# A four-block gated transformer kernel: the cell's sums closed in two planned pieces, queries spread ahead of keys, the first values stored by GpSimd, constants issued behind the gates

## The chip, the cores and the metric

The kernel runs on one core of one Trainium2 chip, in one launch. The metric is the time of an execution on the device in microseconds (us); lower is better.

The names used below: TensorE (PE) multiplies matrices, with its weight loads shown as PEld; VectorE is DVE, ScalarE is ACT, GpSimd is POOL, and SyncE is SP, which here only issues DMAs. SBUF is the on-chip memory, PSUM the accumulator memory that TensorE writes.

## The reference, cut to what matters

Eight sequences of 512 tokens with 256 features pass through four residual blocks, all in float32:

```
x += tanh(g0) * mlstm(layernorm(x), ctx, ctx)          # "cell": 8 heads of 32
x += tanh(f0) * moe_block(layernorm(x))                # self-attention, 32 heads of 8, then 8 experts
x += tanh(g1) * cross_attention(ctx, ctx, layernorm(x))# 16 heads of 16
x += tanh(f1) * product_key_ffn(layernorm(x))          # 4096 experts, top 8 of 64 x 64 per head
```

The cell, for one sequence and head, is

```
ig, fg = gates of [q, k, v];  cs = cumsum(log_sigmoid(fg))
log_D  = cs[s] - cs[t] + ig[t]  for t <= s, else -inf
m      = max_t log_D
C      = (q @ k.T / sqrt(32)) * exp(log_D - m)
h      = (C / (max(|sum_t C|, exp(-m)) + 1e-6)) @ v
out    = layernorm(h over 256 features) * ln_scale
```

The batch norm inside the product-key block takes its mean and variance over all tokens of all sequences, so that block can only start once all eight sequences have left the third one.

## The kernel before, in words

There are two stages. The attention stage (`attention_phase`) does the first three blocks for all sequences, and some matrix products of the fourth ahead. The second stage does the rest of the fourth block.

The attention stage has one backbone: 24 attention jobs of 16 steps. A job ("A", m, f) is one half of the self-attention of the m-th sequence, a job ("C", m, 0) is a cross-attention. Each job is worked through twice: first the maxima (products `sc<-ka,qa`, then a reduction `nm` on VectorE at line 440), then the exponentials (products `sc<-qa,ka`, then `pr` on ScalarE at line 469, then the products `av` at line 485). Normally the maxima of one job and the exponentials of the job before it run in the same step, and each step has two halves. The products of a half have two PSUM buffers (`ps_sc`), so the next half's products must wait until the reduction and the exponential of this half have read theirs. The operands of a job lie in one of three sets (`sets`, tiles `qa` and `ka`), whose rows are filled by `spread` (line 387) with DMAs from a DRAM copy of the projections (`qk_d`). `blank` (line 396) zeroes a row of the queries.

All other work of the attention stage is written as generators, called lanes. A lane yields a cost in planner's microseconds ("this much TensorE work was just issued"), `("wait", t)` ("do not call me for t planner's microseconds"), `("rest", name)` ("not before this name is in the set `rested`") or `("take", True/False)`, which holds or frees the one PSUM bank shared by cell and experts (`ps_ac`, tag "ac"). Behind each half, `beside` (line 1342) calls the first lane that can run until a credit of one or two planner's microseconds is used up. TensorE's instructions stand in exactly the order in which this program issues them (`manual_schedule` with ORDERED). The order on the other engines, SP's DMA queue included, is set by a scheduler, which `tc.issue_after` can hold back.

The lanes that matter here:

- `before` (line 1247) does cell and queries of a sequence. One lane does sequences 0, 2, 3, ... 7 with the tiles of `Tiles`; a second does sequence 1 with the borrowed tiles of `Lent`. Sequence 2 rests on ("cell", 1), which is set when the whole cell of sequence 1 is through.
- `between` (line 1263) calls `begin` (line 957) for each sequence: it rests on ("qk", m), then spreads queries and keys into the set, blanks, and later loads the values `v0` from `vds`.
- `behind` does experts and cross-attention operands, `contexts` keys and values of the cross-attention, `after` what follows it, and `fill` the early products of the fourth block.

`cell` (line 713) works, for sequences 1 to 7, on four pairs of heads one after the other. For each pair it makes the decays (GpSimd line 823, ScalarE line 831), the scores `csc` (line 853), their product with the decays (VectorE line 858) and the sums `cav` (line 838). Then `close` (line 774) copies the sums from PSUM to the SBUF tile `avs` (tag "pk", two buffers, shared with the tiles that carry projections out), transposes `avs` in four pieces into `ht` (line 780), and normalizes on VectorE (lines 785 to 792). For sequence 0, with nothing else to run, `all_pairs` (line 629) does the same in a tighter form and calls the same `close`.

`queries` (line 895) normalizes, projects queries and keys and stores them to `qk_d` through SP (line 927), then projects values and stores them to `v_d` through SP (line 943).

At the start, `lns` (line 281), the scale of the cell's normalization times tanh(g0), is made right after its load, and `constants` (line 324, called at line 739) prepares value tiles, bias and mask.

Of the kernel before, what the change touches and what calls it, by code (L numbers as in the profile page):

```python
# [16 lines left out]
ALU = mybir.AluOpType  # L17
# [19 lines left out]
def kernel(  # L37
# [27 lines left out]
    nc = tc.nc  # L65
# [13 lines left out]
    tg = const.tile([P, 4], F32, name="tg")  # L79
# [100 lines left out]
    def attention_phase(ctx: ExitStack):  # L180
# [97 lines left out]
        lns = cst.tile([P, D], F32, name="lns")  # L278
        nc.scalar.dma_start(lns, ln_scale.partition_broadcast(P))

        nc.vector.tensor_scalar(lns, lns, tg[:, 0:1], None, ALU.mult)


        tbo = cst.tile([P, D], F32, name="tbo")
# [38 lines left out]

        def constants():

            for f in range(2):
                nc.gpsimd.memset(v0[f], 1.0)
            nc.gpsimd.memset(v1, 0.0)
            bo_ps = ps_m.tile([P, S], F32, name="bo_ps", tag="m")
            for k in range(NK):  # L330
                nc.tensor.matmul(
                    bo_ps[:, :D], bqkv_sb[:, 4 + k : 5 + k].to_broadcast([P, P]), wo[:, k, :],
                    start=(k == 0), stop=(k == NK - 1),
                )
            nc.vector.tensor_tensor(tbo, bo_ps[:, :D], tbo, ALU.add)
            nc.vector.tensor_scalar(tbo, tbo, tg[:, 2:3], None, ALU.mult)
            m_f = trp.tile([B * NC, P], F32, name="m_f", tag="pk", bufs=2)
            nc.vector.tensor_copy(m_f, m_u8)
            mp = ps_m.tile([P, S], F32, name="mp", tag="m")
            nc.tensor.transpose(mp[:, : B * NC], m_f, ident[: B * NC, : B * NC])  # L340
            nc.vector.tensor_copy(m_key, mp[:, : B * NC])
            nc.vector.tensor_scalar(m_f, m_f, 1.0, -NEG, ALU.subtract, ALU.mult)
            nc.sync.dma_start(m_dram, m_f)
# [369 lines left out]
        def cell(m, own, loaded):  # L713
# [18 lines left out]
            z, a = rows[:, 1], rows[:, 0]  # L732
            for i, g in ((1, z), (0, a)):
                part = slice(32 * i, 32 * i + 8)
                nc.vector.tensor_scalar(g, gp[part], gb_sb[part], None, ALU.add)
            yield ("take", False)
            yield 0.9
            if m == 0:
                constants()

            nc.scalar.activation(e, z, AF.Abs)
            nc.scalar.activation(e, e, AF.Exp, scale=-1.0)
# [28 lines left out]

            hk = own.tokens("hk")

            def close(pair, av):

                avs = trp.tile([P, S], F32, name="avs", tag="pk", bufs=2)
                nc.any.tensor_copy(avs, av)
                ht = ps_m.tile([P, NC, 2, 2, 32], F32, name="ht", tag="m")
                for c in range(NC):
                    nc.tensor.transpose(  # L780
                        ht[:, c].rearrange("p i w r -> p (i w r)"), avs[:, c * P : (c + 1) * P],
                        ident,
                    )
                dn = small.tile([P, NC, 2], F32, name="dn")
                nc.vector.scalar_tensor_tensor(
                    dn, ht[:, :, :, 1, 0], -1.0, em[:, :, 2 * pair : 2 * pair + 2],
                    ALU.mult, ALU.max,
                )
                nc.vector.tensor_tensor(dn, dn, ht[:, :, :, 1, 0], ALU.max)
                nc.vector.tensor_scalar(dn, dn, EPS_CELL, None, ALU.add)  # L790
                nc.vector.reciprocal(dn, dn)
                nc.vector.tensor_tensor(
                    hk[:, :, 64 * pair : 64 * pair + 64].rearrange("p c (i r) -> p c i r", i=2),
                    ht[:, :, :, 0, :],
                    dn.unsqueeze(3).to_broadcast([P, NC, 2, 32]),
                    ALU.mult,
                )

            if m == 0:
                all_pairs(qT, cT, ce, nM_d, aT, close)  # L800
            mbs = {}

            def fetch_maximum(pair):
# [5 lines left out]
            for pair in range(4) if m else ():  # L809

                if pair not in mbs:
                    fetch_maximum(pair)
                    yield ("wait", 2.5)
                mb = mbs[pair]
                if own.ahead and pair < 3:
                    fetch_maximum(pair + 1)
                g = pair // 2
                pds = {}

                def decay(c):  # L820
                    s0 = c * P

                    nc.gpsimd.affine_select(  # L823
                        out=mb[:, :, s0 : s0 + P], in_=mb[:, :, s0 : s0 + P],
                        pattern=[[0, 2], [1, P]], compare_op=ALU.is_ge,
                        fill=NEG, base=0, channel_multiplier=-1,
                    )
                    pds[c] = own.pair()
                    for i in range(2):
                        h = 2 * pair + i  # L830
                        nc.scalar.activation(  # L831
                            pds[c][:, i, s0:], mb[:, i, s0:], AF.Exp, bias=aT[:, c, h : h + 1]
                        )

                def sums(c):
                    for i in range(2):
                        h = 2 * pair + i
                        nc.tensor.matmul(  # L838
                            av[64 * i : 64 * i + 64, c * P :],
                            ce[:, c, 33 * h : 33 * h + 64],  # L840
                            pds[c][:, i, c * P :], start=(c == 0), stop=(c == NC - 1),
                        )

                decay(0)
                yield ("wait", 1.5)
                yield ("take", True)
                av = own.bank("cav")
                for c in range(NC):
                    s0 = c * P
                    sc = [ps_m.tile([P, S], F32, name="csc", tag="m") for _ in range(2)]  # L850
                    for i in range(2):
                        r = 32 * (2 * (pair % 2) + i)
                        nc.tensor.matmul(
                            sc[i][:, s0:], cT[r : r + 32, g, s0 : s0 + P], qT[r : r + 32, g, s0:],
                            start=True, stop=True,
                        )
                    for i in range(2):
                        nc.vector.scalar_tensor_tensor(  # L858
                            pds[c][:, i, s0:], sc[i][:, s0:], 1.0 / math.sqrt(32.0),
                            pds[c][:, i, s0:], ALU.mult, ALU.mult,  # L860
                        )
                    if c > 0:
                        sums(c - 1)
                    if c < NC - 1:
                        decay(c + 1)
                    yield 1.1 * (NC - c) / NC + (1.1 * (NC + 1 - c) / NC if c else 0)
                    yield ("wait", 1.5)
                sums(NC - 1)
                close(pair, av)
                yield ("take", False)  # L870
                yield 1.1
            Xa = own.stream()
            nc.gpsimd.dma_start(Xa, x[b].rearrange("(c p) d -> p c d", p=P))
            if m == 0:
# [20 lines left out]
        def queries(m, own, Xa):  # L895
# [21 lines left out]
            for i in range(2):  # L917
                w = weights1.get()
                for n in range(NK):
# [7 lines left out]
                        nc.sync.dma_start(pds[i][n * P : (n + 1) * P], pk)  # L927

                    yield from project_T(w, nT, n, store)
            rested.add(("qk", m))  # L930
            vds[m] = drm.tile([P, 2, NC, 16 * 9], F32, name="v_d", bufs=M)
            w = weights1.get()
            for c in range(NC):
                ps = project(w, nT, c)
                pk = trp.tile([P, S], F32, name="vk", tag="pk", bufs=2)[:, : 32 * 9]
                heads = pk.rearrange("p (h e) -> p h e", e=9)
                nc.gpsimd.memset(heads[:, :, 8], 1.0)
                for f in range(2):
                    nc.any.tensor_copy(
                        heads[:, 16 * f : 16 * f + 16, 0:8].rearrange("p (j g) e -> p j g e", g=4),  # L940
                        ps.rearrange("p (j f g e) -> p j f g e", f=2, g=4, e=8)[:, :, f],
                    )
                nc.sync.dma_start(
                    vds[m][:, :, c], pk.rearrange("p (f n) -> p f n", f=2)
                )
                yield 1.0
# [10 lines left out]
        def begin(m):  # L957
            for f in range(2):
                i, last = block2_set(m, f)
                yield ("rest", ("qk", m))  # L960
                if last is None and i:
                    prepare(i)
                if last:
                    yield ("rest", last)
                for half, src in zip(sets[i], qks[m]):
                    spread(half, src, 32 * f, 8)
                blank(sets[i][0])
                yield ("wait", LANDING)
                ready.add(("A", m, f))
                yield ("rest", ("v_d", m))  # L970
# [276 lines left out]
        def before(sequences, tiles):  # L1247
            own, loaded = tiles(), None
            if tiles is Lent:
                loaded = own.begin(sequences[0])  # L1250
                yield ("rest", ("qk", 0))
            for m in sequences:
                if m == 2:
                    yield ("rest", ("cell", 1))
                Xa = yield from cell(m, own, loaded)
                rested.add(("cell", m))
                yield from queries(m, own, Xa)
            if tiles is Lent:
                rested.add(("lent", 0))
# [558 lines left out]
    for g, (p, u) in enumerate(steps):  # L1818
        n, step = g // 8, g % 8
        q = p + 2  # L1820
# [101 lines left out]
```

## Time and profile before

| | |
|---|---|
| times of three runs | 3832.28, 3841.15 and 3819.53 us, median 3832.28 |
| the profiled execution | 3834.04 us, of which the span in the trace is 3832.3 us |
| mean granted TensorE clock | 0.969 of full speed |
| first attention product starts at | 103.81 us |
| closings of the cell, transposes `ht` of cells 1 to 7 | 112 in 28 groups of four, 306 ns each on average |
| copies `avs` | 23 on VectorE (0.68 us typically), 9 on ScalarE (0.56 to 0.59 us) |

How to read it: times in the trace count from the start of the span. Each line of an order of time gives start and duration in us, the engine, the source line, the operation, and what it writes and reads; in square brackets stands how long the engine had been idle before it, and what ended that idle time. A line of a table of waits names the waiting engine and line, what it waited for, then the total in us, the number of times and the longest. A line of windows gives the stretch and its length, then busy us and the number of instructions of PE, PEld, DVE, ACT and POOL, then granted clock, DMA share and GB/s.

### The profile page before, as it was taken

To read this page: it belongs to the slowest core of one execution; us is meant where nothing else is said; L and a number is where in the kernel's file an instruction comes from. 1 tells how busy PE (TensorE), PEld (TensorE's weight loads), DVE (VectorE), ACT (ScalarE), POOL (GpSimd) and SP (SyncE) were. 2 spreads that over 40 slices of the span, in tenths; PEclk is the share of its full clock that TensorE was granted. 3 is DMA by queue.
4 is the path that set the end of the run, shared out by engine and by line. 5 is a ranking of instruction groups with operands and counts; after the bars stand their busy time and mean duration, and the time that the engine had idled before them with its cause. 6 is when DMAs were issued, how large, how long until landed. Compare 5 with 4: busy or idle time off the path is not lost. (4 is left out here: it accounts for less than half of the span.)

```text
span 3832.3 us, 76234 instructions
## 1 busy us (share of the span) xinstructions
PE 3520.6 (92%) x31049; PEld 1837.9 (48%) x31049; DVE 2241.0 (58%) x5490; ACT 1758.3 (46%) x2301; POOL 598.4 (16%) x642
## 2 busy tenths in 40 slices
PE   4788888998999999899999999999899999999998
PEld 2332333443343344334433444434345777777776
DVE  4665555565555555555555543545422689999993
ACT  2125453444445444445445444444443455555551
POOL 3130102121100101101100110100000133333331
PEclk8889999999999999999999999999999999999999
DMA  4331222233322323321332243330434433333331
GB/s 140 104 105 51 63 55 65 59 96 77 97 87 64 87 68 101 87 87 56 104 92 64 71 105 98 92 100 24 136 114 146 124 112 107 107 107 107 107 105 37
DMA packets 226092, 345.35 MB, mean 90 GB/s; under 512 B 25983, under 2 KB 174495, under 8 KB 217439
## 3 DMA queue, kind: packets, MB, share of 16 engines
q1 hardware_dynamic: 207884, 278.02, 24.5%
q0 software_dynamic: 16672, 61.87, 5.4%
q8 instruction: 244, 4.00, 0.4%
q14 instruction: 108, 0.88, 0.1%
q10 hardware_dynamic: 1184, 0.58, 0.1%
HBM read 238.50 MB, written 101.09 MB: 89 GB/s over the span
## 5 line engine op out<-in xcount | busy, mean ns | idle before, releaser
L440 DVE TENSOR_REDUCE nm<-sc 128x2 f32<-128x1024 f32 x768 | 938.7, 1225 | 968.2 <-PE sc L422 967.5
L469 ACT ACTIVATE pr<-sc 128x1024 f32<-128x1024 f32 x768 | 782.8, 1023 | 952.8 <-PE sc L422 952.4
L422 PE MATMUL sc<-ka,qa 32*128 32x512 f32 x3072 | 918.0, 662 | 109.0 <-DVE nm L440 102.9
L422 PE MATMUL sc<-qa,ka 32*128 32x512 f32 x3072 | 866.5, 652 | 17.4 <-ACT pr L469 15.5
L422 PEld LDWEIGHTS sc<-ka,qa 32*128 32x128 f32 x3072 | 250.6, 188 | 458.3 <-DVE nm L440 266.6
L1764 PE MATMUL acc<-up_sb,gs 64*128 64x256 f32 x4096 | 467.9, 381 | 1.3 <-DVE gs L1753 1.3
L131 PE MATMUL ps_hd<-xT,dw 128*64 128x256 f32 x3584 | 435.3, 388 | 14.5 <-DVE pd L858 4.5
L485 PE MATMUL av<-pr,v 128*32 128x512 f32 x3072 | 422.3, 622 | 2.4 <-DMA v<-v_d 2.3
L1764 PEld LDWEIGHTS acc<-up_sb,gs 64*128 64x128 f32 x4096 | 389.8, 187 | 52.2 <-issue 4.9
L131 PEld LDWEIGHTS ps_hd<-xT,dw 128*64 128x64 f32 x3584 | 246.9, 138 | 237.1 <-issue 100.7
L1734 POOL TENSOR_TENSOR m<-o,cwT 128x1024 f32<-128x1024 bf16 x128 | 243.6, 1903 | 581.4 <-DVE o L1732 260.9
L1210 ACT COPY hb<-ps_hd 128x512 f32<-128x512 f32 x224 | 130.9, 585 | 321.2 <-PE ps_hd L131 294.6
L422 PEld LDWEIGHTS sc<-qa,ka 32*128 32x128 f32 x3072 | 234.0, 185 | 53.3 <-ACT pr L469 40.7
L485 PEld LDWEIGHTS av<-pr,v 128*32 128x32 f32 x3072 | 61.3, 109 | 300.5 <-issue 297.1
L831 ACT ACTIVATE pd<-mb,aT 128x512 f32<-128x512 f32 (+1 forms) x224 | 113.5, 554 | 145.7 <-PE cav L838 86.9
L1753 DVE TENSOR_TENSOR gs<-cf,gs 128x1024 f32<-128x1024 f32 x128 | 155.6, 1217 | 41.9 <-PE cf L1744 27.2
L823 POOL TENSOR_SCALAR_AFFINE_SELECT mb<-mb 128x256 f32<-128x256 f32 x112 | 45.3, 406 | 724.9 <-ACT pd L831 407.6
L1744 PE MATMUL cf<-m,m 64*64 64x64 f32 x8192 | 153.1, 222 | 2.7 <-issue 2.0
L1744 PEld LDWEIGHTS cf<-m,m 64*64 64x64 f32 x8192 | 135.3, 135 | 40.8 <-issue 40.4
L1730 ACT CAST m<-o 128x1024 f32<-128x1024 bf16 x128 | 133.7, 1044 | 39.0 <-DVE o L1728 35.2
L1008 PE MATMUL ps_h<-fT,w1e 128*128 128x256 f32 x512 | 135.5, 397 | 8.5 <-DVE o L513 8.0
L1027 PE MATMUL ps_y<-w2e,heT 128*128 128x256 f32 x512 | 131.9, 397 | 0.0
(262 smaller groups left out, 4025.0 us busy)
## 6 DMA issues: line engine op xcount, KB each, us to landing
h_d<-hb SPq DMA_DIRECT2D x224, 256.0 KB
gs<-h_d SPq DMA_DIRECT2D x56, 1024.0 KB
dw<-in_down SPq DMA_DIRECT2D x112, 256.0 KB
w1e<-in_w POOLq DMA_DIRECT2D x16, 1024.0 KB, 5.5
w2e<-in_w POOLq DMA_DIRECT2D x16, 1024.0 KB, 6.5
mb<-nM_d SPq DMA_DIRECT2D x28, 512.0 KB
cT<-in_cxT POOLq DMA_DIRECT2D x22, 512.0 KB, 4.7
qk_d<-pk SPq DMA_DIRECT2D x32, 256.0 KB
```

The lines of the kernel that those rows point to most:

```text
L131: nc.tensor.matmul(ps[64 * q : 64 * q + 64, :], dw[:, k, :], runs[:, :, q, :], start=(k == 0), stop=(k == NK - 1),)
L422: nc.tensor.matmul(sc[:, i, :], lhs[r : r + 32, g, c * P : (c + 1) * P], rhs[r : r + 32, g, :], start=True, stop=True,)
L440: newest = nc.vector.tensor_reduce(self.nm[:, c, 2 * half : 2 * half + 2, g], sc, AX.X, ALU.max, negate=True)
L469: nc.scalar.activation(mine[jj], sc, AF.Exp)
L485: nc.tensor.matmul(self.av[32 * j : 32 * j + 32, :], self.va[:, c, h * (self.hd + 1) : h * (self.hd + 1) + 32], pr[j // 2][:, j % 2, :], s ...
L1008: nc.tensor.matmul(ps[:, :D], w1e[:, k, f * P : (f + 1) * P], fT[:, k, i * D : (i + 1) * D], start=(k == 0), stop=(k == NK - 1),)
L1027: nc.tensor.matmul(py[:, c, :], hT[:, f, c * P : (c + 1) * P], w2e[:, f, :], start=(f == 0), stop=(f == NF - 1),)
L1730: nc.scalar.copy(m1, o1)
L1734: nc.gpsimd.tensor_tensor(m2, o2, tokens(cw), ALU.mult)
L1744: nc.tensor.matmul(cf[64 * q : 64 * q + 64, h, s, :], m2[rows, 4 * q + s // 2, :, s % 2], m1[rows, 4 * q + s // 2, :, s % 2], start=True, ...
L1753: nc.vector.tensor_tensor(gv, cf.rearrange("p h s i -> p i h s"), gv, ALU.mult)
L1764: nc.tensor.matmul(accs[n][q], gs[n % 2][rows, i, :], up_sb[rows, i, :], start=(i == 0), stop=(i == 63),)
```

## The change: what it does

Five edits:

1. `close` is cut in two. `store_sums` copies the sums to `avs`; `close` does transposes and normalizer. For sequences 1 to 7 the lane yields between the two (cost 0.4, then a wait of 1.0), and the shared bank is freed behind the copy as before. Sequence 0 calls both in a row.
2. ("cell", m) is set behind the third pair of the cell (pair 2) instead of behind the whole cell, so the lane of sequence 2 may begin earlier.
3. The projections of queries and keys set ("q", m) and ("k", m) one after the other instead of ("qk", m) behind both. `begin` spreads and blanks the queries behind the first, and spreads the keys behind the second.
4. The values of sequence 0 are stored by a DMA from GpSimd instead of SP.
5. The multiplication of `lns` moves into `constants`, and `constants` is issued behind the second gate's addition (`gated`).

```diff
-        nc.vector.tensor_scalar(lns, lns, tg[:, 0:1], None, ALU.mult)
...
         def constants():
+            nc.vector.tensor_scalar(lns, lns, tg[:, 0:1], None, ALU.mult)
...
-                nc.vector.tensor_scalar(g, gp[part], gb_sb[part], None, ALU.add)
+                gated = nc.vector.tensor_scalar(g, gp[part], gb_sb[part], None, ALU.add)
...
             if m == 0:
-                constants()
+                with tc.issue_after(gated.ins):
+                    constants()
...
-            def close(pair, av):
-
+            def store_sums(av):
                 avs = trp.tile([P, S], F32, name="avs", tag="pk", bufs=2)
                 nc.any.tensor_copy(avs, av)
+                return avs
+
+            def close(pair, avs):
+
                 ht = ps_m.tile([P, NC, 2, 2, 32], F32, name="ht", tag="m")
...
             if m == 0:
-                all_pairs(qT, cT, ce, nM_d, aT, close)
+                all_pairs(qT, cT, ce, nM_d, aT, lambda pair, av: close(pair, store_sums(av)))
...
                 sums(NC - 1)
-                close(pair, av)
+                avs = store_sums(av)
                 yield ("take", False)
-                yield 1.1
+                yield 0.4
+                yield ("wait", 1.0)
+                close(pair, avs)
+                yield 0.7
+                if pair == 2:
+                    rested.add(("cell", m))
...
                     yield from project_T(w, nT, n, store)
-            rested.add(("qk", m))
+                rested.add(("qk"[i], m))
...
-                nc.sync.dma_start(
+                (nc.sync if m else nc.gpsimd).dma_start(
                     vds[m][:, :, c], pk.rearrange("p (f n) -> p f n", f=2)
                 )
...
-                yield ("rest", ("qk", m))
+                yield ("rest", ("q", m))
...
-                for half, src in zip(sets[i], qks[m]):
+                for half, src, name in zip(sets[i], qks[m], "qk"):
+                    yield ("rest", (name, m))
                     spread(half, src, 32 * f, 8)
-                blank(sets[i][0])
+                    if name == "q":
+                        blank(half)
...
-                yield ("rest", ("qk", 0))
+                yield ("rest", ("k", 0))
...
                 Xa = yield from cell(m, own, loaded)
-                rested.add(("cell", m))
                 yield from queries(m, own, Xa)
```

## The prediction

> **What bounds the kernel now.** I read the page first (busy shares, slices, chain), then windows of time, then what ends the idle time of TensorE, then the order of time at two places the change touches.
>
> ```profile
> span 3832.3 us, 76234 instructions
> PE 3520.6 (92%) x31049; PEld 1837.9 (48%) x31049; DVE 2241.0 (58%) x5490; ACT 1758.3 (46%) x2301; POOL 598.4 (16%) x642
> ...
> 0.00:104.00 104.00, 49.06 (x230) 25.66 (x231) 42.31 (x105) 27.30 (x54) 37.01 (x59) 0.81 0.46 136
> 104.00:150.00 46.00, 36.85 (x119) 17.18 (x120) 29.08 (x40) 8.22 (x13) 4.43 (x9) 0.69 0.41 106
> 150.00:250.00 100.00, 80.97 (x358) 38.11 (x357) 61.85 (x106) 20.43 (x37) 16.94 (x33) 0.83 0.28 85
> 250.00:500.00 250.00, 217.00 (x1340) 83.65 (x1336) 154.78 (x248) 116.78 (x151) 43.42 (x69) 0.97 0.23 69
> ```
>
> TensorE is the bound (92%). Its idle time is 312 us: 55 lie before 104 us, where the first attention product starts, and most of the rest in the attention stage up to 2680 us. There the waits of TensorE are:
>
> ```profile
> PE sc L422 <- DVE nm L440: 86.9, 158, 4.8
> PE ht L780 <- DVE avs L777: 26.5, 21, 1.9
> PE sc L422 <- ACT pr L469: 15.5, 15, 2.6
> PE ht L780 <- ACT avs L777: 7.6, 7, 1.7
> ```
>
> (us in total, times, longest, from 150 to 2680 us.) The second and fourth rows are one place in the code: the 28 closings of the cells 1 to 7, where the transposes `ht` stand directly behind the last sums, so that TensorE idles for the copy between them: 26.5 + 7.6 = 34.0 us (rounded rows), 1.21 us each. One of them in order of time:
>
> ```profile
> 341.57 1.23 DVE L440 TENSOR_REDUCE nm<-sc 128x2 f32<-128x1024 f32 x1 [1.12 <-PE sc L422]
> ...
> 342.03 0.44 PE L838 MATMUL cav<-pd,cte 128*64 128x128 f32 x4
> ...
> 342.87 0.63 DVE L777 COPY avs<-cav 128x512 f32<-128x512 f32 x1
> ...
> 343.56 0.66 PE L780 MATMUL ht<-ident,avs 128*128 128x128 f32 x4 [1.09 <-DVE avs L777]
> ...
> 344.14 0.69 PE L422 MATMUL sc<-ka,qa 32*128 32x512 f32 x1
> ```
>
> The start-up, by the two chains that the change meets:
>
> ```profile
> 13.10 0.35 DVE L281 TENSOR_SCALAR lns<-lns,tg 128x256 f32<-128x256 f32 x1 [5.26 <-DMA lns<-in_ln_scale]
> ...
> 14.27 1.14 ACT L228 COPY cte<-cx 128x512 f32<-128x512 f32 x2 [10.01 <-DMA cx<-in_cx]
> 15.43 1.31 ACT L360 COPY qT<-ps_t 128x512 f32<-128x512 f32 x2
> ...
> 92.09 0.32 SPq L927 DMA_DIRECT2D qk_d<-pk  x1
> 95.89 0.64 SPq L943 DMA_DIRECT2D v_d<-vk  x1
> 96.58 2.28 SPq L391 DMA_DIRECT2D qa<-qk_d  x3
> 98.91 1.79 SPq L391 DMA_DIRECT2D ka<-qk_d  x4
> ...
> 103.81 4.29 PE L422 MATMUL sc<-ka,qa 32*128 32x512 f32 x8 [5.28 <-DMA ka<-qk_d]
> ```
>
> **What the Trainium skill says.** Perfetto Trace Analysis, "Identifying the Most-Contended Engine", warns that matmul busy share does not show nearness to the roofline and asks for the share of weight loads too: here 92% beside 48%, so I count only gaps whose releaser is named. The same page, "Optimization Strategy", says a gap that repeats on the engine that should be saturated points at buffers or at what signals it; the 28 gaps of 1.21 us are such a series, and their releaser is a copy, not a missing buffer. DMA: Bandwidth & Descriptors, "Issuing engines are not separate DMA queues", says another issuing engine saves only issue time, since the transfers share the same DMA engines. The trace agrees on the size (0.64 us for the store) but shows more at stake: the store's place in SP's queue, behind a wait of 3.5 us. "Latency and other measured facts" of that page puts the fixed cost of a DMA near 2 us; here a `qk_d` store takes 4.6 us until its buffer is free (92.09 to the wait's end near 96.7), and 4.6 is used.
>
> **The change part by part.**
>
> 1. Constants behind the gates. The multiplication of `lns` stands ahead of the first normalization on VectorE and holds it to 13.37 us, though `rs` is ready at 9.69. Moving it frees 3.7 us there, but the next step, the copy of `qT`, follows on ScalarE's queue behind L228, which waits for `cx` and ends at 15.41. The copy starts at 15.43 either way: worth 0. Were `cx` early, up to 3.7. The constants' VectorE work then runs between 23.4 and 25.1 us, under the wait for the logarithm (25.90): 0.35 + 0.40 + 0.18 + 0.17 + 0.35 + 0.21 = 1.7 of 2.5 us. Cost 0.
>
> 2. Queries ahead of keys, values by GpSimd. In the new SP order the four query spreads stand in front of the second key store, the values are gone, then come the key spreads. The first two can go at 91.1; the other two need the second query store (87.70 + 4.6 = 92.3), so four at 0.39 end near 93.1. The second key store slips from 92.09 to 93.1, lands at 97.7, and only then go the last two key spreads: 97.7 and 98.1. Before, the last of four in 1.79 us went near 100.2. The first product moves up by about 2 us (103.8 to 101.8). Should spreads cost 0.76 each, as the three at 96.58 did, 0.5 us remains; with no contention 3. I take -2. The value stores on GpSimd have no row; nearest are its loads at 0.76 to 0.85 us issue and 5 us landing, so the fourth lands near 109, where the load of `v0` went before (109.27). SP waits there with the spreads of set 1 behind it, until about 113; set 1 is first read after the 16 steps of the first job, near 210 us, and `v0` by the first `av` at 244.6. Cost 0.
>
> 3. Copy and transposes in two pieces, 28 times. In the new TensorE order every `ht` of cells 1 to 7 has at least one group of attention products or four projections between it and the last sums, so the copy (0.63) is covered and the 34.0 us go. What is late next is the maxima (L440): the stall also gave VectorE time. In the example the reduction ends at 342.80 and the last sums at 342.47; without stall and `ht`, the next products start at 342.80: a wait of 0.33 replaces 1.09, so 0.76 of 1.09, 70%, is kept: 34.0 x 0.70 = 23.8 us. Bounds: none is kept if the maxima bind in each such half (0), or all of it plus `ht` itself filling gaps of about 0.42 us before products elsewhere (28 x 0.42 = 12): -46. I take -24.
>
> 4. Cell 2 may start after pair 2 of cell 1. Before the 64th group of four attention products 30 more other matmuls stand than before, where TensorE is only 80% busy; the total work is the same, and the last 82 groups of four products and all behind them stand in the same order. Attention steps that run with only one of the two kinds of product: 50 before, 48 after. The price for cell 1: counted in eights of attention products, its last key projection stands behind 18.5 of them instead of 17.5 (an eight takes some 6 us there), and job (A, 1, 0) needs it behind 22.5. Before, the spreads were issued by 295.1, landed by about 300, and the products began near 321: 20 us of room, so 14 remain. Cost 0, between -6 and +6 for the reshuffled order.
>
> Sum against the profiled span: 3832.3 - 2 - 24 = 3806. The run with the profile took 3834.0, the median of the three shown is 3832.3, so no correction is made.
>
> **Rivals.**
>
> A. The forecast: 3806, own range 3794 to 3818.
>
> B. The stall becomes a wait for the maxima. For it: L440 is already the largest releaser (86.9 us, 158 times), and a half-step with nothing beside it takes 2.47 us by that loop (346.70 to 349.17). Against: the new order puts other products into these halves. A quarter of the 34 kept and the 2 of the start: 3832 - 8.5 - 2 = 3822.
>
> C. The transposes fill gaps as well as lose theirs, and the early cell 2 fills the start: -46 at the extreme, about -38: 3794.
>
> D. Slower. The stall was the shadow in which VectorE did copy and normalizer; now the copy (0.63) and the chain of five small operations behind `ht` (344.25 to 345.51, 1.26) stand between two reductions. If every close falls into a half bound by the maxima it costs 28 x 1.89 = 53 us against 34 + 2 saved: +17, 3849, and more with a waiting `dn` ahead of a reduction. It outweighs the gain once more than 19 of 28 closes (36 / 1.89) lie in such halves. Only 158 of some 700 halves wait for the maxima today, and six of the copies move to ScalarE (23 to 17 on VectorE), so I hold it unlikely.
>
> That the change does not do what it says is excluded for the split (the order shows it) and is what I forecast for the constants.
>
> **How the numbers follow.** A 0.55, B 0.23, C 0.10, D 0.12. A change of 0.5% is 19 us, so faster means below 3813 and slower above 3851. A holds about 0.47 of faster, C 0.10, B 0.03 and measuring spread (the three runs lie within 22 us) leaves it there: 0.60 faster. Slower is the upper part of D, 0.09, where the spread of runs counts; the rest, 0.31, is within. The range takes A and C whole and B up to its upper end: 3790 to 3834.
>
> **What would show each step.** Right: TensorE's wait at `ht` for `avs` falls from 34 to under 4 us; the wait of L422 on L440 grows by about 10, not 30; the first product of `sc` at 101.8; `qT` copied at 15.4 still; no wait of products for `ka` of set 2. Wrong: L422 on L440 above 115 us (B, D); first products near 98 (constants mattered) or beyond 103; a gap on `ka<-qk_d` near 320. The forecast fails as a whole if TensorE's busy time itself moves, say by the granted clock.

## The result and the profile after

| | before | after |
|---|---|---|
| median, 16 runs each on the same chip | 3827.9 us | 3814.85 us |
| smallest to largest | 3818.01 to 3841.15 | 3803.85 to 3826.14 |
| span of the profiled run | 3832.3 us | 3820.4 us |
| TensorE idle in it (span less busy) | 311.7 us | 299.3 us |

The ratio is 0.9966, 95% interval 0.9953 to 0.9979: 13 us, about half of the gain that was forecast. It is a real gain (the interval excludes 1), and the median lies inside the forecast range of 3790 to 3834. But it is smaller than the 0.5% from which the prediction counts a kernel as faster, which it held more likely than not (0.60). The page of after:

```profile
span 3820.4 us, 76232 instructions
PE 3521.1 (92%) x31049; PEld 1833.6 (48%) x31049; DVE 2246.6 (59%) x5491; ACT 1756.5 (46%) x2300; POOL 600.5 (16%) x646
```

TensorE's busy time did not move (3520.6 before), so the 12 us between the two profiles are idle time of TensorE. The waits of TensorE in after from 150 to 2680 us (total, times, longest):

```profile
PE sc L422 <- DVE nm L440: 102.3, 169, 4.2
PE sc L422 <- ACT pr L469: 19.0, 16, 2.6
...
PE ht L784 <- DVE nT L355: 1.1, 1, 1.1
PE ht L784 <- ACT avs L777: 0.4, 1, 0.4
```

The stall at `ht` is gone: 34.0 us became 0.4, or 1.5 with the one wait for another tile. The waits for the maxima grew from 86.9 to 102.3 and those for the exponentials from 15.5 to 19.0: together 19 us, more than half of the 34. One close in order of time, in after:

```profile
357.07 0.44 PE L842 MATMUL cav<-pd,cte 128*64 128x128 f32 x4
357.47 0.69 PE L422 MATMUL sc<-ka,qa 32*128 32x512 f32 x1
...
357.58 0.58 ACT L777 COPY avs<-cav 128x512 f32<-128x512 f32 x1 [0.26 <-PE cav L842]
...
358.55 0.66 PE L784 MATMUL ht<-ident,avs 128*128 128x128 f32 x4
358.67 1.23 DVE L440 TENSOR_REDUCE nm<-sc 128x2 f32<-128x1024 f32 x1 [1.25 <-PE sc L422]
...
359.95 0.69 PE L422 MATMUL sc<-ka,qa 32*128 32x512 f32 x1 [0.75 <-DVE nm L440]
```

The copy runs beside a group of attention products, and `ht` starts without a bracket: TensorE was not idle before it. The following products wait 0.75 us for a reduction that nothing had delayed: this half-step has only `ht` (0.66) beside a reduction of 1.23. What such a place costs depends on what else stands in its half-step.

The stretches that were shown of before, in after:

```profile
0.00:104.00 104.00, 51.78 (x225) 26.43 (x225) 43.35 (x105) 26.21 (x50) 36.87 (x58) 0.78 0.46 134
104.00:150.00 46.00, 34.28 (x117) 15.51 (x117) 26.73 (x38) 6.96 (x14) 5.68 (x11) 0.69 0.46 112
150.00:250.00 100.00, 85.80 (x351) 39.96 (x348) 62.71 (x109) 20.53 (x39) 14.85 (x32) 0.78 0.27 83
250.00:500.00 250.00, 213.99 (x1292) 82.82 (x1284) 150.62 (x245) 113.26 (x148) 47.40 (x71) 0.96 0.24 70
```

From 250 to 500 us TensorE idles 36.0 us, more than the 33.0 of before, although four of its 28 closes fall there in either kernel. The gain lies later, from 500 to 1500 us (81.4 us idle before, 65.4 after), and part of it is lost again from 2200 to 2600 us, where no close is left (the last `ht` of before starts at 2129 us, that of after at 2146; 15.6 us idle before, 23.8 after). A change of what stands where in TensorE's order shows itself far from the lines that were edited.

The start, by SP's and GpSimd's DMAs and the value tiles:

```profile
94.38 1.42 SPq L391 DMA_DIRECT2D qa<-qk_d  x4
...
95.89 0.34 SPq L936 DMA_DIRECT2D qk_d<-pk  x1
...
98.58 4.65 SPq L391 DMA_DIRECT2D ka<-qk_d  x4
98.60 0.56 ACT L948 COPY vk<-ps_q 128x128 f32<-128x128 f32 x2 [7.57 <-DMA qk_d<-pk]
...
99.72 0.68 POOL L953 DMA_DIRECT2D v_d<-vk  x1 [0.94 <-ACT vk L948]
...
105.56 0.56 ACT L948 COPY vk<-ps_q 128x128 f32<-128x128 f32 x2 [6.40 <-DMA v_d<-vk]
...
106.18 2.08 PE L381 MATMUL ps_q<-ws,nT 128*128 128x256 f32 x4 [4.89 <-ACT vk L948]
...
108.18 2.09 PE L422 MATMUL sc<-ka,qa 32*128 32x512 f32 x8
```

SP's order is the one that was forecast: four query spreads, the second key store, the key spreads. But the first attention product starts at 108.18 us, not at 101.8. The second value tile waits until the store of the first has landed, 5.8 us after its issue, and the values' projections stand ahead of the first attention products in TensorE's order.

### The profile page after: what moved, and what is told of

Its sections match the earlier page's. It is cut to its first block, busy times and chain, and to the rows that moved or that the text cites. A ratio compares the mean times of both kernels' runs of the same rounds, so it can differ in the third digit from the quotient of the medians.

```text
span 3820.4 us, 76232 instructions
## 1 busy us (share of the span) xinstructions
PE 3521.1 (92%) x31049; PEld 1833.6 (48%) x31049; DVE 2246.6 (59%) x5491; ACT 1756.5 (46%) x2300; POOL 600.5 (16%) x646
## 4 chain that ended last, share of the span: by engine, by line
PE 78%; DVE 10%; ACT 2%; issue 2%; DMA 1%; POOL 0%; SPq 0%; DVEq 0%; ACTq 0%; POOLq 0%
PE sc L422 22%; PE acc L1775 12%; PE ps_hd L131 10%; PE av L485 7%; DVE nm L440 7%; PE cf L1755 4%; PE ps_y L1039 3%; PE ps_sim L1507 3%; PE ps_q L381 3%; PE ps_h L1020 3%; PE ps_p L370 2%; PE cav L842 2%; PE csc L857 2%; PE ps_hl L131 1%; PE ps_t L351 1%
## 5 line engine op out<-in xcount | busy, mean ns | idle before, releaser
L440 DVE TENSOR_REDUCE nm<-sc 128x2 f32<-128x1024 f32 x768 | 938.9, 1225 | 953.6 <-PE sc L422 952.3
L422 PE MATMUL sc<-ka,qa 32*128 32x512 f32 x3072 | 913.0, 661 | 117.7 <-DVE nm L440 117.3
L422 PE MATMUL sc<-qa,ka 32*128 32x512 f32 x3072 | 864.9, 651 | 20.8 <-ACT pr L469 19.0
L422 PEld LDWEIGHTS sc<-ka,qa 32*128 32x128 f32 x3072 | 247.0, 187 | 462.4 <-DVE nm L440 275.0
L422 PEld LDWEIGHTS sc<-qa,ka 32*128 32x128 f32 x3072 | 233.1, 185 | 59.8 <-ACT pr L469 45.4
L1741 ACT CAST m<-o 128x1024 f32<-128x1024 bf16 x128 | 133.7, 1045 | 39.3 <-DVE o L1739 35.5
```

What stands on the lines that cost most here:

```text
L422: nc.tensor.matmul(sc[:, i, :], lhs[r : r + 32, g, c * P : (c + 1) * P], rhs[r : r + 32, g, :], start=True, stop=True,)
L440: newest = nc.vector.tensor_reduce(self.nm[:, c, 2 * half : 2 * half + 2, g], sc, AX.X, ALU.max, negate=True)
L1741: nc.scalar.copy(m1, o1)
```

## The experiments

Twelve kernels were run, each beside the kernel before on the same chip. The edits keep the numbers of the list above; "edit 2 alone" is the kernel before with that edit. (All but e10 are made from after. Where edit 3 is undone there, `blank` still stands ahead of the key spreads in SP's queue; in before and e10 it stands behind them. No other difference remains.) Two counts are quoted beside the times, both taken from TensorE's instruction order, not from a trace: steps in which the maxima or the exponentials run alone (for each kind), and half-steps with next to no filling, here called near-empty (under 0.5 us of other products, `av` included, by their usual durations, between one group of products `sc` and the next; half-steps 21 to 700). The last column is explained below the table.

| kernel | ratio, 95% interval | alone | near-empty | wait for maxima, us | time less that of before at equal clock, us |
|---|---|---|---|---|---|
| before | 1 | 25 | 20 | 86.9 | 0 |
| after | 0.9966 (0.9953 to 0.9979) | 24 | 16 | 102.3 | -17 |
| e1: edits 1, 2 | 0.9941 (0.9918 to 0.9964) | 25 | 16 | 102.7 | -22 |
| e2: edits 2 to 5 | 1.0068 (1.0048 to 1.0088) | 26 | 25 | 106.0 | +13 |
| e3: all but edit 4 | 0.9971 (0.9958 to 0.9984) | 24 | 16 | 101.6 | -17 |
| e4: all but edit 5 | 0.9971 (0.9960 to 0.9982) | 24 | 16 | 101.1 | -17 |
| e5: edit 2 | 1.0047 (1.0030 to 1.0065) | 26 | 25 | 106.5 | +10 |
| e6: edit 3 | 1.0007 (0.9993 to 1.0021) | 25 | 17 | 85.3 | 0 |
| e7: edit 1 | 1.0039 (1.0025 to 1.0053) | 36 | 26 | 117.9 | +9 |
| e8: edits 1, 2, and 3 for the first sequence | 0.9926 (0.9905 to 0.9946) | 25 | 16 | 100.6 | -24 |
| e9: as e1, another stated cost | 1.0049 (1.0032 to 1.0066) | 36 | 28 | 105.0 | +13 |
| e10: before, other stated costs | 1.0101 (1.0067 to 1.0136) | 36 | 28 | 117.3 | +30 |
| e11: edits 1, 3, 4, 5 | 0.9969 (0.9958 to 0.9980) | 26 | 20 | 108.7 | -12 |
| e12: as e8, another stated cost | 0.9916 (0.9884 to 0.9948) | 26 | 12 | 88.1 | -35 |

Most of the scatter between runs of one kernel goes with the mean granted clock of TensorE, which each run has on record. The 101 runs of before that stood beside the experiments took 3837 us on average where the clock was 0.968, 3831 at 0.970, 3820 at 0.973 and 3815 at 0.975: some 3 us for each 0.001. The kernels differ in their mean clock too, from 0.968 (e2, e5, e10) to 0.972 (e1, e8, and before), and those with the same order of TensorE's products agree in it within 0.001 (e1 and e8; after, e3 and e4). Whether the order brings its clock with it was not tested. The last column takes the clock out by one straight line for all kernels. It is an estimate, good to some 3 us, and where it differs much from the ratio the text gives both.

**e1, the cut and the early release of cell 2.** Edits 3 to 5 are undone.

```diff
-                rested.add(("qk"[i], m))
+            rested.update({("q", m), ("k", m)})
...
-                (nc.sync if m else nc.gpsimd).dma_start(
+                nc.sync.dma_start(
```

> The kernel before with the two-piece close and the earlier release of cell 2, without the three start edits. Theory T (split is worth some 17 us, start edits cost 3 to 4): 3828 - 17 = about 3811, first attention product at 104 +- 1.5 us, wait of ht for avs under 2 us, wait of products on the maxima up by about 15 us. Rival R (start edits are neutral, the later start of the changed profile is scatter): 3815, as the changed kernel.

Measured: 3798.18 against 3822.53 us. No wait at `ht` for `avs` above 1.5 us is left. The gain, 23 us by the ratio, is larger than either theory gave, but the interval (14 to 31 us) takes in the 17 us of theory T, and it overlaps that of after. It was a hint that something in edits 3 to 5 takes some of the gain away again, not more.

**e2, everything but the cut.**

```diff
-                avs = store_sums(av)
+                close(pair, store_sums(av))
                 yield ("take", False)
-                yield 0.4
-                yield ("wait", 1.0)
-                close(pair, avs)
-                yield 0.7
+                yield 1.1
```

> The changed kernel with copy and transposes in one piece again; all else changed. T: 34 us of waits at ht are back, the waits on the maxima are back near 87, first product at 107 to 108: about 3831, slower than before by 3. R: 3828, equal to before. If the gain came from the earlier cell 2 and not from the split: about 3816.

Measured: 3847.5 us, slower than before (by 13 us at equal clock), and outside every theory. The waits at `ht` are there (31.4 us), but those for the maxima rose to 106.0 all the same. So they do not need the cut in order to grow. This is where the theory "the stall is handed over to the maxima" began to fail.

**e3, the values stored by SP again**, with the other edits kept.

```diff
-                (nc.sync if m else nc.gpsimd).dma_start(
+                nc.sync.dma_start(
```

> The changed kernel with the values of sequence 0 stored by SyncE again. T: the chain of value stores on one buffer no longer holds the projections ahead of the first product, first product 2 to 4 us earlier relative to the query projections than in the changed kernel, about 3812. R: no change, 3815.

Measured: 3811.46 us, ratio 0.9971 (0.9958 to 0.9984), the same as after. The start by itself did move:

```profile
98.66 0.64 SPq L953 DMA_DIRECT2D v_d<-vk  x1
99.34 2.24 SPq L391 DMA_DIRECT2D ka<-qk_d  x4
...
100.63 0.56 ACT L948 COPY vk<-ps_q 128x128 f32<-128x128 f32 x2 [2.05 <-DMA ws<-in_w]
...
102.18 0.56 ACT L948 COPY vk<-ps_q 128x128 f32<-128x128 f32 x2 [0.99 <-DMA v_d<-vk]
...
103.25 4.14 PE L422 MATMUL sc<-ka,qa 32*128 32x512 f32 x8
```

Here the second value tile does not wait for the first one's store (it takes the other buffer of the tag "pk"), and the third waits 3.5 us after that store's issue. In the changed kernel every value tile of sequence 0 waits for the store of the tile just before it: all four go through one buffer, where in before and e3 they take two by turns. The first query projection begins anywhere from 80.3 to 86.3 us in these profiles, which no edit explains. So the start is compared from that projection to the first attention product: 20.6 to 22.8 us in the six kernels with neither edit 3 nor 4 (before, e1, e5, e7, e9, e10; mean 21.6), 20.2 to 21.3 in the four with queries ahead and SP's stores (e3, e6, e8, e12; mean 20.8), and 23.4 to 24.3 in the four with GpSimd's stores as well (after, e2, e4, e11; mean 23.7). The 3 us lost by GpSimd's stores are not seen in the time of the whole run, whose interval would hide them.

**e4, the constants ahead again**, with the other edits kept.

```diff
-            nc.vector.tensor_scalar(lns, lns, tg[:, 0:1], None, ALU.mult)
...
-                with tc.issue_after(gated.ins):
-                    constants()
+                constants()
```

> The changed kernel with lns and the constants at their old place. T: no gap between the first transposes and the gate products, the gate products on the context take 2.3 us instead of 3.2, worth 1 us: 3814. R: nothing, 3815. In both the copy of qT follows the copy of the keys on ScalarE.

Measured: 3810.56 us, ratio 0.9971 (0.9960 to 0.9982). The edit is worth nothing that can be measured.

**e5, edit 2 alone.** By now the theory was that the order of TensorE's filling work moves the time by itself.

```diff
+                if pair == 2:
+                    rested.add(("cell", m))
...
                 Xa = yield from cell(m, own, loaded)
-                rested.add(("cell", m))
```

> The kernel before with only the earlier release of cell 2. Theory T2 (moving a lane's start re-deals the filling work of all later half-steps, and that alone is worth as much as the stalls): 25 halves with next to no filling instead of 20, as in the kernel without the split; about 3840, slower by 15 to 25 us, waits on the maxima above 100 us, waits at ht still 34. Rival (the slowness of the kernel without the split came from its start edits): 3822, as before.

Measured: 3844.34 against 3824.96 us, 18 us slower by the ratio, 10 at equal clock. It repeats the waits of e2: 106.5 us for the maxima, 22.8 for the exponentials (one of 9.1), 31.4 at `ht`, and one of 5.0 on the load of `wkv`. TensorE's order is that of e2 but for 60 of 16165 places. So most of what e2 loses comes with edit 2, a release that adds no work.

**e6, edit 3 alone** (a diff as in the change, with the values left to SP).

> The kernel before with only the queries released ahead of the keys, for all sequences. T2: 17 halves with next to no filling, about as before, within 6 us of it: 3816 to 3828; at the start, first product some 2 us earlier after the first projection (20.2 instead of 22). Rival: this edit is what made the kernel without the split slow: above 3838.

Measured: 3831.95 us, no difference. The waits for the maxima stay at 85.3 us and those at `ht` at 36.5.

**e7, edit 1 alone**, in `cell`:

```diff
-                close(pair, av)
+                avs = store_sums(av)
                 yield ("take", False)
-                yield 1.1
+                yield 0.4
+                yield ("wait", 1.0)
+                close(pair, avs)
+                yield 0.7
```

> The kernel before with only the two-piece close. T2: waits at ht fall from 34 to about 1 us, but the re-dealt order has 36 steps with only one kind of product instead of 25 and 26 halves with next to no filling, so part of it is lost: 3810 to 3822. Rival (the split carries the whole gain of 24 us seen with the earlier cell 2): 3799.

Measured: 3838.88 us, slower than before, where both theories expected a gain. TensorE's waits:

```profile
PE sc L423 <- DVE nm L441: 117.9, 175, 5.4
PE sc L423 <- ACT pr L470: 17.4, 18, 2.3
...
PE ht L784 <- ACT avs L777: 1.1, 1, 1.1
```

The 34 us at `ht` went, as intended, and 31 us came at the maxima. The loss has a place: from 2200 to 2600 us, first in before, then in e7 (window, length, then busy PE).

```profile
2200.00:2600.00 400.00, 384.38 (x2748) 171.92 (x2744) 184.42 (x226) 182.96 (x218) 30.71 (x34) 1.00 0.34 96
```

```profile
2200.00:2600.00 400.00, 360.51 (x2520) 159.06 (x2520) 176.59 (x226) 166.43 (x201) 25.39 (x29) 0.98 0.31 88
```

TensorE idles 39.5 us instead of 15.6, in a stretch without any close; 26.2 of them are waits for the maxima, 9.7 in before. Its order has 36 steps of each kind alone, instead of 25. What was open: is that loss the order's, or does the cut bring it by what it does on VectorE?

**e8, edits 1 and 2, with edit 3 for the first sequence only.**

```diff
-                rested.add(("qk"[i], m))
+                if m == 0:
+                    rested.add(("qk"[i], m))
...
+            rested.update({("q", m), ("k", m)})
```

> Split and earlier cell 2, and for sequence 0 alone the queries ahead of the keys, values by SyncE, constants at their old place. TensorE's order is that of the first experiment, instruction for instruction; only the order of DMAs at the start differs. Expected: first product 1 to 2 us earlier after the first projection than there, and the time of the first experiment less 0 to 2: ratio to before 0.993 to 0.994. Would the queries ahead of the keys matter more than their start, it would differ from it by over 5 us.

Measured: 3801.33 us, like e1, from which it cannot be told apart. Its interval lies below that of after. Edits 4 and 5 are worth nothing by e3 and e4, where TensorE's order is that of after. So what after loses against e8 (0.0040, 15 us; 7 at equal clock) comes with edit 3 in the sequences 1 to 7, of whose new order the prediction said nothing. In the kernel before the same edit costs nothing (e6).

**e9 and e10, nothing but stated costs.** No work is added or removed in either, but more than TensorE's order is dealt anew: copies that VectorE or ScalarE may do are given out afresh. Of the 32 copies `avs` VectorE does 17 in e1 and 24 in e9. The first takes e1 and changes one number, the second takes the kernel before and states the three costs of the cut around a `close` that stays whole:

```diff
                 close(pair, avs)
-                yield 0.7
+                yield 0.9
```

```diff
                 close(pair, av)
                 yield ("take", False)
-                yield 1.1
+                yield 0.4
+                yield ("wait", 1.0)
+                yield 0.7
```

> As the first experiment (edits 1 and 2, ratio 0.9941), but the cost that the lane states behind the transposes is 0.9 instead of 0.7: no instruction is added, removed or changed, only the order in which TensorE's filling work falls between the half-steps. Counted in the order: 36 steps of each kind run alone instead of 25, and 28 half-steps have next to no filling instead of 16. Theory O (how the filling work is dealt out sets the time): near the kernel with the cut alone, which has 36 and 26: about 1.004, 3840 us, waits on the maxima near 118 us, idle time in 2200 to 2600 us near 40 us, still no wait at ht. Rival M (the cut and the early release of cell 2 set the time by what they do themselves): as the first experiment, 0.994, 3800 us, waits on the maxima near 103.

> The kernel before, with the costs that the lane states behind close changed alone: 0.4, a wait of 1.0 and 0.7 in place of 1.1. close itself stays whole, so the 34 us of waits at ht stay. No instruction is added or removed. In the order 36 steps of each kind run alone (25 before) and 28 half-steps have next to no filling (20 before). Theory O: the cut alone cost 15 us although it removed 34 us of stalls, so its order costs some 49 us; here the order is alike and the stalls stay: about 3870 us, ratio 1.012, waits on the maxima near 115. Rival M: nothing was done, so 1.000, 3825 us, waits on the maxima near 87.

Measured: e9 3845.32 us and e10 3865.65 us, with before at 3825.35. One number costs 41 us in e9 against e1 (ratios 1.0049 and 0.9941; 34 at equal clock), and the stated costs alone cost 39 us in e10 (ratio 1.0101; 30 at equal clock). Rival M, for which nothing had been done, falls in both. Of theory O's signs for e9 the idle time from 2200 to 2600 us came, 39.3 us where e1 has 22.1 (first e1, then e9):

```profile
2200.00:2600.00 400.00, 377.87 (x2638) 167.04 (x2639) 179.10 (x221) 183.03 (x210) 19.55 (x23) 0.98 0.30 87
```

```profile
2200.00:2600.00 400.00, 360.67 (x2544) 161.26 (x2540) 171.70 (x232) 160.86 (x197) 27.25 (x32) 0.98 0.32 92
```

The wait for the maxima near 118 did not come: it is 105.0, hardly more than the 102.7 of e1. In the waits of e10 the maxima grow as in e7, and `ht` keeps its stall:

```profile
PE sc L422 <- DVE nm L440: 117.3, 176, 5.6
PE ht L780 <- DVE avs L777: 26.3, 21, 2.5
PE sc L422 <- ACT pr L469: 11.6, 13, 2.3
...
PE ht L780 <- ACT avs L777: 7.6, 7, 2.4
```

e7 and e10 are a pair. With the transposes `ht` left out, their 16037 other products stand in the same order, one by one. What differs is the cut, besides the place of `blank` and three copies that other engines do. Its worth in this order: ratio 1.0039 against 1.0101, that is 0.62%, 24 us, with the two intervals added in squares from 9 to 38 us. At equal clock it is 21 us, give or take some 4. (The two profiled spans, 3830.6 and 3868.2 us, lie further apart.) The 33.9 us at `ht` go to 1.1 and the maxima stay at 117.9 against 117.3: in the same order the removed stall is not handed over to them.

How the order can cost time is seen in e9 around 2560 us, where half-steps stand with no filling but `av`, or with none:

```profile
2558.08 1.23 DVE L441 TENSOR_REDUCE nm<-sc 128x2 f32<-128x1024 f32 x1 [0.76 <-PE sc L423]
...
2559.37 0.69 PE L423 MATMUL sc<-ka,qa 32*128 32x512 f32 x1 [0.34 <-DVE nm L441]
...
2560.56 1.23 DVE L441 TENSOR_REDUCE nm<-sc 128x2 f32<-128x1024 f32 x1 [1.25 <-PE sc L423]
...
2561.84 0.69 PE L423 MATMUL sc<-ka,qa 32*128 32x512 f32 x1 [1.33 <-DVE nm L441]
```

and beside it a half-step of e10 that has some:

```profile
2555.85 1.95 PE L131 MATMUL ps_hd<-xT,dw 128*64 128x256 f32 x16
2556.02 1.23 DVE L440 TENSOR_REDUCE nm<-sc 128x2 f32<-128x1024 f32 x1 [2.72 <-PE sc L422]
...
2557.73 0.69 PE L422 MATMUL sc<-ka,qa 32*128 32x512 f32 x1
```

With 1.95 us of filling the reduction ends 0.48 us before its successor needs it. With none, TensorE stands for 1.33 us, or 0.34 where products `av` follow, and the loop takes 2.47 us. Filling work that was given to another half-step, in which TensorE had no idle time to fill, then costs its whole duration there.

**e11, all but the early release of cell 2.** Edit 2 undone in after:

```diff
-                if pair == 2:
-                    rested.add(("cell", m))
...
                 Xa = yield from cell(m, own, loaded)
+                rested.add(("cell", m))
```

> The kernel after with edit 2 alone undone: cell 2 rests on the whole of cell 1 again. 26 steps alone of each kind, 20 half-steps with next to no filling (after: 24 and 16). Theory O: edit 2 matters only through the order; with counts near those of the kernel before but without the stalls at ht, about 3820 us, 0.998 to 1.000. Rival E (the early release of cell 2 is what makes the cut pay): near the kernel with the cut alone, 1.004, 3838 us. Rival N (edit 2 is worth nothing): as after, 0.9966, 3813 us.

Measured: 3815.29 us, as after (rival N), and 4 to 12 us better than theory O put it by its counts. At equal clock it is 5 us slower than after. So an edit that costs 18 us (10 at equal clock) in the kernel before costs nothing here, and may gain a little: its price belongs to the order it meets, not to the edit. The counts give the direction, not a time to a few us.

**e12, one more stated cost**, chosen for the fewest near-empty half-steps among the costs whose order was counted.

```diff
                 close(pair, avs)
-                yield 0.7
+                yield 1.2
```

> As the eighth experiment (edits 1 and 2, and edit 3 for the first sequence alone, ratio 0.9926), with the stated cost behind the transposes 1.2 instead of 0.7. 26 steps alone of each kind, 12 half-steps with next to no filling (16 there). Theory O, if the half-steps without filling are what counts: 5 to 10 us under the eighth, about 0.991, 3793 us. Rival M: no change, 0.9926, 3801 us. If the steps alone count as well, they weigh one more, which is within what can be measured.

Measured: 3793.05 against 3825.35 us, the best of all kernels, 32 us under the kernel before and, by the ratios, 19 us under after. Against e8 the ratio differs by 0.0010, 4 us, with intervals that overlap; at equal clock e12 is faster by 11 us, near the 5 to 10 expected. The waits:

```profile
PE sc L423 <- DVE nm L441: 88.1, 150, 4.8
PE sc L423 <- ACT pr L470: 28.4, 19, 10.9
```

The maxima are back near their old 86.9 us, without the stall at `ht`. A single wait of 10.9 us for the exponentials is left, whose cause was not looked into.

## Why the prediction was half right

**Constants behind the gates: 0.** Right. The copy of `qT` starts right behind the copy of line 228 in after too, though at 17.16 us and not at 15.4, since line 228 waits there until 16.00 for the load of `cx`. And e4 measures no difference.

**Queries ahead: −2; value stores on GpSimd: 0.** The first half has the right sign, but the mean gain is 0.8 us and the kernels overlap. It lies near the lower end of 0.5 that the prediction kept for slow spreads. The second is wrong. The prediction asked when the last store would land and who reads `v0`. It did not ask for what the issuing engine changes in the buffers: with the stores on GpSimd each value tile waits for the landing of the one before it, and the projections behind these tiles stand ahead of the first attention product. The cost at the first product is 3 us, below what the whole run shows. The load of `v0` goes at 117.35 us, not near 109. The sign named for a miss here, a first product beyond 103, came.

**The cut: −24.** Right where it can be seen by itself. The pair of e7 and e10 gives 24 us with a wide interval, 21 at equal clock, for 28 closes in an otherwise equal order. The share kept by the profiles' idle time is 29.3 of 34 us (345.5 to 316.2). The predicted wait at `ht` under 4 us is right, and "L422 on L440 grows by about 10, not 30" is off in the number (15). As e2 and e5 show, this wait grows without the cut too, so it was no sign of the cut at all.

**The reshuffled order: 0, between −6 and +6.** This step failed, and the sum came out at twice the measured gain. It priced the new order by the count of steps alone (50 to 48 of both kinds) and by equal total work, and gave it to edit 2 only. The runs show three things. The costs that the cut states (0.4, a wait of 1.0, 0.7) deal all later filling work anew, and alone cost 39 us (30 at equal clock). Edit 2 alone costs 18 (10). And edit 3 reorders the sequences 1 to 7, some 15 us (7) when e8 is set against after. These do not add up: in the order of after the net price of all re-dealing, with the start, is by subtraction what is missing in the sum, 26 forecast less 13 measured, 13 us. No product waited for `ka` of set 2 in after, so the 14 us of room held. A bound of 6 us to either side was too narrow for every one of them. That the time still fell inside the range was partly luck: the order of after is one of the cheap ones. With the same cut alone, in another order, e7 is 15 us slower than before and outside the range.

**The rivals.** B (3822, the stall becomes a wait for the maxima) came nearer to the gain than the forecast of 3806: 10 us in B and 26 in the forecast, against 13 measured. Its mechanism is refuted by e7 and e10 in the order that these two share. In the order of after the wait did grow by 15 us, but it grows by 19 in e2, which has no cut. C (3794) was too far on the other side. D (VectorE's copy and normalizer between the reductions) was not seen: the wait for the maxima does not grow when the cut is made in an equal order.

**Open.** That the new deal costs the time is shown; how it does is shown only in part. The near-empty count follows the time well (12, 16, 20, 26, 28 against 0.9916, 0.9926 to 0.9971, 0.9969, 1.0039, 1.0049 among kernels with the cut), but it is a description, first used for e5, and not a sum. Even at 1.33 us each, the 12 more near-empty half-steps of e9 against e1 come to 16 us, an estimate that is less than half of the 34 to 41 measured. e9 is as slow as e7 with 13 us less of waits for the maxima, and loses 7.6 us to the loads of `dw` and more to waits for VectorE elsewhere. How much a given half-step loses was not worked out, nor what the clock adds. What the copies that change engine cost was not separated from the order either; the number of `avs` copies on VectorE does not set the time, since e12, the fastest, has 25 there.

## What to carry to other kernels

Where filling work is dealt out by stated costs and then stands in a fixed order, an edit to one lane is two changes: what it does, and a new deal for all that comes after. Separate them before a verdict, with a run that has the new costs and the old code: here the code gained 24 us and the deal lost 39 (21 and 30 at equal clock), and a useful cut looked like a loss by itself. Then treat the stated costs as parameters to be tuned, since one number moved this kernel by 41 us. Before a difference of a few us is explained, look at the granted clock of the runs: here 15 us became 7 at equal clock. And when a store moves to another engine, look at which buffer the next tile waits for, not only at the issue time.

## What the runs showed of the hardware

The four value stores of GpSimd, 144 KB each, take 0.67 to 0.68 us to issue and land after 2.3 to 5.7 us, median 2.9. The Trainium skill, DMA: Bandwidth & Descriptors, "Anatomy of one DMA — SWDGE (gpsimd) path", fits a fixed 2.0 us plus the bytes at 436 GB/s, which gives an estimate of 2.3 us for 144 KB. The trace agrees at its minimum, not at its longest. That one, the first store, was issued while the key spreads were under way, and it is the one which counted.

The first query projection starts up to 6 us apart between profiles (80.3 to 86.3), with no edit that goes with it. A gain of 2 us at the start cannot be read from one profile each.

In runs of one and the same kernel the time follows the mean granted clock: in the 101 runs of before the clock lies between 0.967 and 0.976 and the time between 3840 and 3810 us, and about a straight line of some 3 us for each 0.001 the runs scatter by 2.6 us, instead of 7.1 about their mean.
